# The first 489 steps of a delta-rule pipeline in an order of their own, and the preparation of the second sequence two slots earlier

## The chip, the cores and the metric

The kernel runs on one core of a Trainium2 chip. A core has five engines with instruction streams of their own, each in order: TensorE (PE; its weight loads are shown apart as PEld), VectorE (DVE), ScalarE (ACT), GpSimd (POOL) and SyncE (SP), which here issues all transfers. The metric is the device time of one execution in microseconds (us); smaller is better. Several executions are timed and the median is given; one more is profiled, and all traces come from that one.

## The reference

The input has 4 sequences of 512 rows of 256 numbers, all float32. Each sequence is normalized (layer norm). A gated delta-rule attention follows: the rows are projected to q, k, v and z, a causal convolution of four taps and a silu go over q, k and v, and per head a recurrence runs over the sequence in chunks. There are 16 q/k heads, and each serves two of the 32 v heads; a head has 128 channels. Beside it stand two numbers per row and head, beta (a sigmoid) and g (a decay), the "gates". In a chunk

```python
decay = jnp.where(tril, jnp.exp(g[..., :, None] - g[..., None, :]), 0.0)
M = jnp.where(stril, jnp.einsum('bhncd,bhnmd->bhncm', k_beta, k) * decay, 0.0)
T = solve_triangular(eye + M, eye, lower=True)
v_new = v_i - jnp.einsum('bhcd,bhde->bhce', kcd_i, state)
state = state * jnp.exp(g_last)[..., None, None] + ...
```

so every chunk needs the inverse of a triangular matrix and the state that the chunk before it left. The heads' results are normalized, multiplied by silu(z) and projected back to 256 channels (`s`). A feed-forward network whose weights are looked up in a table of 16 numbers gives `g`; the output is `x + s * silu(g)`.

## The kernel before, in words

The work is cut into 64 items: 4 sequences times 16 q/k heads, with the two v heads of each, numbered 0 to 63. An item's 512 rows are 4 chunks of 128. An item consists of some 115 named steps, each a few instructions; `STEPS` holds them. Those that matter here, in the order in which an item needs them:

- `gk`, `gq`, `gv0`, `gv1`, `gz`, `go` load weights; `g` loads the item's rows of g into the tile ds, `e` loads exp(g) into qe. These are SP's, and SP issues in order, so an issue that waits for a free buffer holds all later ones.
- `ak`, `aq`, `av0`, `av1` (L444) project on PE, `yk`... (L450) copy the last tap out on ACT, `ck0`...`cv12` (L456) are the other taps on DVE, `sk`... (L92) the silu on ACT. `z0`, `z1` project z (L478).
- `tk`, `tq`, `tv0`, `tv1` transpose on PE (L510), `sqk`, `sqq` sum squares on ACT (L503), `lk` (L88) takes logarithm and exponentials of them. Changes between the exp and the silu functions cost ACT a table load (L86, L92).
- `ds` (L495, DVE), `ls`, `x0`, `x1` (L88, ACT) make the decay; `kk0`, `kk1` (L556, PE) the products; `nt0`, `nt1` and `at0`, `at1` (L564, DVE) multiply both; `am` (L577, GpSimd) masks at; `qm` (L599, GpSimd) multiplies q into qe. `po`, which reads them, waits for both.
- The inverse: `nd` and `nl` (SP) bring the 32x32 diagonal blocks of nt through memory into a layout with one block row per partition; `yl` (ACT) sets the identity; `L0` to `L3` (L633 and L639, GpSimd) are 31 substitutions of two instructions, 62 in all; `yd` and `iu` (SP) bring the result back; `tp` (L660, DVE) transposes it; merge 1 (`m1`: W on PE L672, `wt` on ACT, U on PE L675, `iu2` on ACT, `t10` on DVE) and merge 2 (`m2`: W2 L703, `w2`, U2 L705, `iu4`) join the blocks to the inverse of 128x128. In `m1` the W of one item and the U of the item before it are interleaved instruction by instruction, in `m2` likewise.
- The recurrence: `ks`, `r`, `pv`, `vn`, `ps`, `st` and `po` for the four chunks (L729, L738, L746, L753, L759, L766, L778 and L781); then `sqo`, `so`, `ro`, `o`, `th`, `h`, and the output projection `pp0`, `pp1` (L824) with its sum `ac0`, `ac1` (L836) on DVE.

The items are pipelined by a string `SLOT` of 122 entries. Entry `pp1:13` says that slot n does step pp1 of item n - 13; `ak:1` that it does ak of item n - 1. A slot thus does one item's worth of work, taken from up to 14 items, and there are 64 slots and 14 more. The first slots have few steps, because the items that they would serve do not exist yet. The order in which the steps are called is written down, and at the end of the kernel every instruction is tied to the one before it on its engine: each engine runs in exactly that order, and one that waits holds all behind it.

Two other things are mixed in. An `X` in the string does one step of the table lookup of the feed-forward weights (two DVE instructions, L334 and L333; `lookups()` begins a new table with L326 to L330 and stores the old one), from slot 6 on; there are four a slot. A `Y` adds one to `due`, and `prepare()`, called behind every step, does one part of the preparation of the next sequence as long as `due` is above zero and two memory banks are free: `normed` (load of x, statistics on DVE, rs on ACT, scaling on DVE, transposes on PE L213, copy on ACT, a store) and then `gated` (ba on PE L233, softplus on DVE and ACT, the running sum gsum on PE, exponentials on ACT, gT on PE, and stores of g and exp(g) into memory). The preparation of sequence b + 1 begins at item 8 of sequence b; that of sequence 0's gates is spread over the first steps.

Every tile has a number of buffers (`NBUF`): two for wk, yl, nl and yd, three for nt and v1, four for q and qe, five for at and kd, nine for k, one where nothing is said (wq, the loads of v, ds, r and the lookup's tiles).

Of the kernel before, what the change touches and what calls it, by code (L numbers as in the profile page):

```python
# [15 lines left out]
B, S, D = 4, 512, 256  # L16
HQK, HV, HD = 16, 32, 128
# [21 lines left out]
def gated_delta_ffn_kernel(  # L39
# [359 lines left out]
    STEPS = {}  # L399
# [266 lines left out]
    def merge1(it, pred):  # L666
        pu = pred and pred.put("pU")[:, : G * Q].rearrange("p (g i) -> p g i", g=G)
        pw = it and it.put("pW")[:, : G * Q].rearrange("p (g i) -> p g i", g=G)
        for g in range(G):
            if it:  # L670
                for lo, hi in HALVES:
                    nc.tensor.matmul(pw[hi, g, :], lhsT=it.nt[lo, g, hi], rhs=it.tpl[lo, g, :Q], start=True, stop=True)  # L672
            if pred:
                for lo, hi in HALVES:
                    nc.tensor.matmul(  # L675
                        pu[lo, g, :], lhsT=pred.wt[hi, g, :], rhs=pred.iut[hi, g, hi], start=True, stop=True
                    )
# [20 lines left out]
    def merge2(it, pred):  # L698
        pu = pred and pred.put("pU2").rearrange("p (g i) -> p g i", g=G)
        pw = it and it.put("pW2").rearrange("p (g i) -> p g i", g=G)  # L700
        for g in range(G):
            if it:
                nc.tensor.matmul(pw[HI, g, :], lhsT=it.nt[LO, g, HI], rhs=it.tpl[LO, g, :], start=True, stop=True)  # L703
            if pred:
                nc.tensor.matmul(  # L705
                    pu[LO, g, :], lhsT=pred.w64[HI, g, :], rhs=pred.iut[HI, g, HI], start=True, stop=True
                )
# [146 lines left out]
    def feed_forward():  # L854
# [125 lines left out]
        "av0:6 at0:5 ck2:1 tv0:8 yl:5 at1:5 sqo0:10 ps0:9 yv0:6 st0:9 cv00:6 th1:11 nl:5 L3:6 av1:4 "  # L980
        "th0:11 sqo1:10 yd:6 vt0:8 tv1:7 am:9 h1:11 cv01:6"
    )
    plan = [(name, int(lag or 0)) for name, _, lag in (key.partition(":") for key in SLOT.split())]
    MERGES = {"m1": merge1, "m2": merge2}
    lags = dict(plan)
    last_lag = max(lag + (name in MERGES) for name, lag in plan)
    total = HQK * B
    looked = lookups()
    preparing = gated(0)
# [5 lines left out]
    spare, needed = 0, None  # L995
    traced = nc.cur_bb.bb.instructions
    begin = traced[-1]
    items, kept, slot = [], [], 0

    def item(n):  # L1000
        return items[n] if 0 <= n < total else None

    def feed():

        nonlocal spare, needed
        while needed is not None and spare >= needed and len(free) > 2:
            spare -= needed
            needed = next(feeding, None)

    def both(b):  # L1010
        yield from normed(b)
        yield from gated(b)

    due = 0

    def prepare():

        nonlocal due
        if due and len(free) > 1:
            due -= 1  # L1020
            while next(preparing, None):
                pass

    for n in range(total + last_lag):
        if n < total:
            items.append(Item(n))
            b, hq = divmod(n, HQK)
            if hq == HQK // 2 and b + 1 < B:
                for _ in preparing:
                    pass  # L1030
                due = 0
                preparing = both(b + 1)
        if n == total + 6:
            for _ in looked:
                pass
            needed = next(feeding)
        slot = n
        for name, lag in plan:
            if name == "X":
                if n >= 6:  # L1040
                    next(looked, None)
            elif name == "Y":
                due += 1
            elif name in MERGES:
                if item(n - lag) or item(n - lag - 1):
                    MERGES[name](item(n - lag), item(n - lag - 1))
            elif item(n - lag):
                STEPS[name](item(n - lag))
                due += n < 4 and name[0] in "ac"
                prepare()  # L1050
            elif needed is not None:
                spare += PASSES.get(name, 0)
                feed()
    slot = total + last_lag
# [53 lines left out]
```

## Time and profile before

| | us |
|---|---|
| median of three timed executions | 2072.44 (2071.39 to 2076.25) |
| the profiled execution | 2075.89 |
| its span in the trace | 2073.7 |
| PE busy | 1969.2 |
| DVE busy | 1775.5 |
| ACT busy | 1621.0 |
| GpSimd busy | 1388.5 |
| first substitution of item 0 (L633) | at 53.9 |
| first output projection (L824) | at 246.5 |
| last substitution (item 63, L639) | at 1860.3 |

Busy times are unions over an engine's instructions and leave out the short pauses between them: GpSimd's 62 instructions of an item are busy for some 19 us and take 23 to 24. The profiled execution took 3.45 us more than the median. In rows of instructions the columns are the start, the duration, the engine, the line, the operation, what it writes and reads, and in brackets the idle time before it with what ended it. In a list of waits the three numbers are the total, the count and the longest. In a table of stretches each engine has its busy time and its number of instructions, then come the granted clock of PE, the share of the transfer engines and GB/s.

### The profile page before, as it was taken

The page shows a single profiled execution, that of the slowest core. Times are in us where ns is not written, and L with a number is a line of the kernel's source. Part 1 is how long each engine was busy: PE and PEld are TensorE (multiplying, and loading weights), DVE is VectorE, ACT ScalarE, POOL GpSimd, SP SyncE. Part 2 cuts the span into 40 slices and gives each one's busy share as a digit, 9 for nine tenths or more (in the row PEclk, how much of TensorE's full clock was granted, in tenths as well). Part 3 has the DMA queues.
Part 4 walks back from the last instruction along what each step waited for, and adds up shares of the span by engine and source line. Part 5 has one row for each costly group of instructions (what it writes and reads, how often), then busy time and mean ns, then how long its engine had stood idle before and what let it go on. Part 6 is the DMA issues. An engine that isn't in the chain of part 4 may idle for free.

```text
span 2073.7 us, 48691 instructions
## 1 busy us (share of the span) xinstructions
PE 1969.2 (95%) x15744; PEld 1442.6 (70%) x15744; DVE 1775.5 (86%) x4356; ACT 1621.0 (78%) x4689; POOL 1388.5 (67%) x4181
## 2 busy tenths in 40 slices
PE   6468999999999999999999999999999999998999
PEld 3235777777777777777777777777777777775755
DVE  7788999999999999999998999999999988862323
ACT  5467889888888888888888888888888989963321
POOL 0777777777777767777777767777777777780000
PEclk9779999999999999999999999999999999999999
DMA  2343443344433444334443344443344343321211
GB/s 76 98 107 89 123 106 103 96 108 120 116 103 100 105 111 105 104 100 110 123 108 101 91 119 103 112 105 102 97 113 123 104 108 100 100 75 44 71 51 51
DMA packets 371885, 206.40 MB, mean 100 GB/s; under 512 B 224544, under 2 KB 353712, under 8 KB 371632
## 3 DMA queue, kind: packets, MB, share of 16 engines
q1 hardware_dynamic: 371632, 203.29, 37.3%
q8 instruction: 126, 2.06, 0.4%
q14 instruction: 127, 1.04, 0.2%
HBM read 179.05 MB, written 24.13 MB: 98 GB/s over the span
## 4 chain that ended last, share of the span: by engine, by line
PE 73%; DVE 16%; POOL 3%; ACT 3%; DMA 3%; issue 1%; SPq 1%; DVEq 0%; POOLq 0%; ACTq 0%
PE av L444 9%; PE pp L824 8%; PE pz L478 7%; PE pv L746 5%; PE po L781 4%; PE ak L444 4%; PE pgu L907 4%; PE kk L556 4%; PE po L778 3%; PE aq L444 3%; PE ps L759 3%; PE ks L729 3%; PE th L510 2%; PE pW L703 2%; PE ptv L510 2%; DVE v L456 2%
## 5 line engine op out<-in xcount | busy, mean ns | idle before, releaser
L633 POOL TENSOR_TENSOR pr<-nl,yl 128x60 f32<-128x60 f32 (+24 forms) x1984 | 584.0, 294 | 220.7 <-ACT ik L88 47.6
L639 POOL TENSOR_TENSOR yl<-yl,pr 128x60 f32<-128x60 f32 (+24 forms) x1984 | 605.1, 305 | 155.7 <-DMA yd<-yl 0.4
L456 DVE SCALAR_TENSOR_TENSOR v<-av,cw,v 128x509 f32<-128x509 f32 (+2 forms) x384 | 282.4, 735 | 0.6 <-ACT v L450 0.3
L478 PE MATMUL pz<-xnT,wz 128*128 128x512 f32 x512 | 242.4, 596 | 4.4 <-DVE acc L836 2.5
L824 PE MATMUL pp<-wo,zT 128*128 128x256 f32 x1024 | 243.7, 381 | 0.5 <-DVE zT L816 0.2
L444 PE MATMUL av<-xnT,wv 128*128 128x512 f32 x512 | 241.3, 594 | 1.4 <-DMA wv<-in_w_qkvz 1.4
L824 PEld LDWEIGHTS pp<-wo,zT 128*128 128x128 f32 x1024 | 185.0, 190 | 25.2 <-issue 2.9
L599 POOL TENSOR_TENSOR qe<-qe,q 128x384 f32<-128x384 f32 x128 | 126.3, 1008 | 100.6 <-DMA qe<-eg_rows 52.3
L86 ACT ACT_TABLE_LOAD x128 | 164.2, 1283 | 3.1 <-PEq L1098 0.8
L92 ACT ACT_TABLE_LOAD x128 | 164.2, 1283 | 2.3
L88 ACT ACTIVATE ds<-ds,ls 128x128 f32<-128x128 f32 x512 | 156.9, 390 | 8.2 <-DVE ls L532 6.6
L738 DVE SCALAR_TENSOR_TENSOR r<-ks,neg,vt 128x128 f32<-128x128 f32 x384 | 116.0, 343 | 44.7 <-PE ks L729 42.9
L456 DVE SCALAR_TENSOR_TENSOR q<-aq,cw,q 128x509 f32<-128x509 f32 (+2 forms) x192 | 142.3, 741 | 13.1 <-ACT q L450 10.8
L503 ACT ACTIVATE junk_o<-po 128x128 f32<-128x128 f32 x512 | 142.1, 278 | 14.3 <-PE po L781 2.1
L478 PEld LDWEIGHTS pz<-xnT,wz 128*128 128x128 f32 x512 | 95.5, 190 | 78.8 <-issue 61.2
L456 DVE SCALAR_TENSOR_TENSOR k<-ak,cw,k 128x509 f32<-128x509 f32 (+2 forms) x192 | 141.4, 736 | 2.0 <-ACT k L450 1.6
L746 PEld LDWEIGHTS pv<-r,iut 128*128 128x128 f32 x768 | 105.6, 191 | 46.0 <-issue 38.2
L444 PE MATMUL ak<-xnT,wk 128*128 128x512 f32 x256 | 135.1, 653 | 0.5 <-DMA wk<-in_w_qkvz 0.5
L444 PEld LDWEIGHTS av<-xnT,wv 128*128 128x128 f32 x512 | 87.6, 191 | 65.6 <-issue 63.9
L746 PE MATMUL pv<-r,iut 128*128 128x128 f32 x768 | 124.8, 285 | 8.4 <-DVE r L738 7.5
L444 PE MATMUL aq<-xnT,wq 128*128 128x512 f32 x256 | 120.7, 594 | 2.8 <-DMA wq<-in_w_qkvz 1.8
L495 DVE TENSOR_SCALAR ds<-ds,gc 128x128 f32<-128x128 f32 x512 | 120.9, 305 | 2.0
(177 smaller groups left out, 5058.1 us busy)
## 6 DMA issues: line engine op xcount, KB each, us to landing
ds<-g_rows SPq DMA_DIRECT2D x64, 512.0 KB, 4.0
nl<-nd SPq DMA_DIRECT2D x256, 128.0 KB, 3.9
qe<-eg_rows SPq DMA_DIRECT2D x64, 384.0 KB, 4.3
wv<-in_w_qkvz SPq DMA_DIRECT2D x128, 128.0 KB, 2.4
wz<-in_w_qkvz SPq DMA_DIRECT2D x64, 256.0 KB, 2.8
wo<-in_w_out SPq DMA_DIRECT2D x64, 256.0 KB, 3.1
wk<-in_w_qkvz SPq DMA_DIRECT2D x64, 128.0 KB, 2.5
wq<-in_w_qkvz SPq DMA_DIRECT2D x64, 128.0 KB, 2.3
```

The lines of the kernel that those rows point to most:

```text
L86: nc.scalar.preload_act_table_set("natural_log_exp_and_others")
L88: nc.scalar.activation(out, in_, func, **kw)
L92: nc.scalar.activation(out, in_, AF.Silu)
L444: nc.tensor.matmul(ps, lhsT=getattr(it, "w" + x)[:, d, :], rhs=it.xnT[:, d, :], start=(d == 0), stop=(d == DC - 1),)
L456: nc.vector.scalar_tensor_tensor(y[:, sh:], ps[:, : S - sh], cw[:, block(it.hq), j : j + 1], y[:, sh:], ALU.mult, ALU.add)
L478: nc.tensor.matmul(ps, lhsT=it.wz[:, d, p * P : (p + 1) * P], rhs=it.xnT[:, d, :], start=(d == 0), stop=(d == DC - 1),)
L503: nc.scalar.activation(junk, ps[:, c, :], AF.Square, accum_out=out[:, c : c + 1])
L599: nc.gpsimd.tensor_tensor(it.qe[:, p], it.qe[:, p], thirds(it.q, NC)[:, 1:, :], ALU.mult)
L633: nc.gpsimd.tensor_tensor(pr[:, :k, :n], nl[:, j : j + 1, j + 1 :].to_broadcast([R * LH, k, n]), yl[:, :k, j : j + 1].to_broadcast([R * LH ...
L639: nc.gpsimd.tensor_tensor(yl[:, :k, j + 1 :], yl[:, :k, j + 1 :], pr[:, :k, :n], ALU.subtract)
L746: nc.tensor.matmul(pv[:, p, :], lhsT=it.iut[:, p * NC + c, :], rhs=it.r[:, p, :] if c else vt[:, c, :], start=True, stop=True,)
L824: nc.tensor.matmul(ps[:, j, :], lhsT=chunk(hT, 2 * c2 + j), rhs=it.wo[:, p, :], start=(p == 0), stop=(p == NP - 1),)
```

## The change

A second string, `FRONT`, names 489 steps with the item of each (`L2:4` is the third part of the substitutions of item 4). They are done ahead of the loop over slots, in that order; the loop then leaves out what is done. FRONT covers about what slots 0 to 10 did and parts of 11 to 13: k of items 0 to 7, substitutions up to the third part of item 4, item 0 up to `pp1` and `ac1`. The merges are named by halves there (W, U, W2, U2), so the first W and U of items 0 to 2 stand alone and are not interleaved. The loads of `gk`, `gq`, `gv0`, `gv1`, `gz` and `go` of item 0 and `gk` of item 1 come first of all, and `yl` of items 0 and 1; `ak` of item 0 comes ahead of ba. On GpSimd qm and am of item 0 come ahead of the first substitution, qm of items 1 and 2 behind item 0's substitutions, qm of item 3 behind item 1's, am of item 1 behind item 3's. No lookup step is in FRONT.

After FRONT the loop begins at slot 0; slots 0 to 8 have no step left, slot 9 has 5, slot 10 has 13, slot 11 has 58 of 112, slot 12 has 105 of 114, and from slot 14 on all are as before. Slots 6 to 8 therefore emit their twelve lookup steps in a row. The preparation of sequence 1 begins at slot 6 instead of 8; as `prepare()` is called behind steps only, the counts of slots 6 to 8 add up and a part goes behind each step from slot 9 on. The gates of sequence 0 go behind the steps 9 to 39 of FRONT. The common order begins, on DVE, at the instruction that started at 293.7 us of the profiled execution. The number of instructions is the same on all engines but ACT, which has 252 table loads where it had 256.

```diff
+    FRONT = (
+        "yl:0 gk:0 yl:1 gk:1 gq:0 gv1:0 gv0:0 gz:0 ak:0 go:0 aq:0 yk:0 gk:2 ck0:0 ck1:0 ak:1 yq:0 gq:1 "
+        "ck2:0 cq0:0 sk:0 cq1:0 av1:0 yk:1 gk:3 cq2:0 ck0:1 sq:0 ck1:1 aq:1 yv1:0 gv1:1 ck2:1 cv10:0 sk:1 "
+        "cv11:0 kk1:0 yq:1 gq:2 cv12:0 cq0:1 tq:0 sv1:0 tk:0 cq1:1 sqq:0 ak:2 cq2:1 sqk:0 eq:0 aq:2 gk:4 "
+        "yk:2 g:0 sq:1 ck0:2 e:0 kk0:0 ck1:2 e:1 yq:2 ck2:2 gq:3 kk1:1 e:2 cq0:2 sk:2 e:3 cq1:2 av1:1 cq2:2 "
+        "lk:0 ls:0 ds:0 tq:1 yv1:1 gv1:2 tk:1 sqq:1 qm:0 ak:3 kd:0 cv10:1 sqk:1 cv11:1 kk0:1 gk:5 cv12:1 "
+        "yk:3 aq:3 eq:1 lk:1 ck0:3 x0:0 ck1:3 x1:0 ck2:3 av0:0 gq:4 yq:3 nt1:0 nt0:0 tk:2 ls:1 nd:0 at1:0 "
...
+        "po0:1 yv1:6 nd:5 po1:1 vn2:1 cv10:6 yl:5 ps2:1 cv11:6 sqo0:1 po2:1 cv12:6 iu:3 st2:1 L1:4 tq:6 "
+        "sv1:6 so0:1 ks3:1 sqq:6 tv0:3 r3:1 U2:2 nl:5 vt0:3 pv3:1 vt1:3 pp1:0 ds:6 iu4:2 vn3:1 gv1:7 tp:3 "
+        "av0:4 ro0:1 L2:4 ac1:0"
+    )
     plan = [(name, int(lag or 0)) for name, _, lag in (key.partition(":") for key in SLOT.split())]
     MERGES = {"m1": merge1, "m2": merge2}
+    HALF = {"m1": ("W", "U"), "m2": ("W2", "U2")}
+    STEPS.update({
+        "W": lambda it: merge1(it, None), "U": lambda it: merge1(None, it),
+        "W2": lambda it: merge2(it, None), "U2": lambda it: merge2(None, it),
+    })
...
+    for name, _, m in (key.partition(":") for key in FRONT.split()):
+        m = int(m)
+        while len(items) <= m:
+            items.append(Item(len(items)))
+        if (name, m) == ("g", 0):
+            for _ in preparing:
+                pass
+        done.add((name, m))
+        STEPS[name](items[m])
+        due += 8 < len(done) < 40
+        prepare()
     for n in range(total + last_lag):
...
-            if hq == HQK // 2 and b + 1 < B:
+            if hq == (HQK // 2 if b else 6) and b + 1 < B:
...
             elif name in MERGES:
-                if item(n - lag) or item(n - lag - 1):
-                    MERGES[name](item(n - lag), item(n - lag - 1))
-            elif item(n - lag):
+                it, pred = (
+                    None if (half, m) in done else item(m) for half, m in zip(HALF[name], (n - lag, n - lag - 1))
+                )
+                if it or pred:
+                    MERGES[name](it, pred)
+            elif item(n - lag) and (name, n - lag) not in done:
                 STEPS[name](item(n - lag))
-                due += n < 4 and name[0] in "ac"
                 prepare()
```

## The prediction

> **What bounds the kernel now.** First the page: totals and slices.
>
> ```profile
> PE 1969.2 (95%) x15744; PEld 1442.6 (70%) x15744; DVE 1775.5 (86%) x4356; ACT 1621.0 (78%) x4689; POOL 1388.5 (67%) x4181
> ...
> PE   6468999999999999999999999999999999998999
> PEld 3235777777777777777777777777777777775755
> DVE  7788999999999999999998999999999988862323
> POOL 0777777777777767777777767777777777780000
> ```
>
> The reader is to see that PE is full from slice 4 on, DVE too, and that only the first four slices (207 us) have room. So next the stretches of the start, and two stretches of four steady slots each behind them:
>
> ```profile
> core 0: us, PE busy (x) PEld busy (x) DVE busy (x) ACT busy (x) POOL busy (x), PEclk, DMA share, GB/s
> 25.00:54.00 29.00, 24.50 (x77) 12.82 (x78) 23.28 (x45) 22.08 (x58) 0.12 (x1) 0.88 0.35 96
> 54.00:168.00 114.00, 59.08 (x410) 35.33 (x408) 86.86 (x207) 59.18 (x166) 90.85 (x280) 0.78 0.41 105
> 168.00:257.00 89.00, 84.23 (x714) 63.43 (x714) 80.66 (x207) 76.75 (x222) 67.38 (x203) 0.97 0.39 99
> 257.00:346.00 89.00, 86.97 (x789) 64.76 (x789) 84.48 (x213) 76.02 (x222) 66.51 (x198) 1.00 0.41 107
> 346.00:458.00 112.00, 111.56 (x913) 83.52 (x900) 108.29 (x265) 98.60 (x288) 86.21 (x257) 1.00 0.41 105
> ```
>
> From 168 us on PE and DVE are both at 91 to 99%. PE paces a slot at 28 us (112 / 4), DVE needs 27.1 of them, so DVE can make up about 1 us a slot and no more. PE's room lies in 54:168, 55 us of it; DVE has 27 us there. What holds PE in that stretch is in the waits of the first 300 us:
>
> ```profile
> POOL pr L633 <- ACT ik L88: 47.6, 1, 47.6
> PEld pW L672 <- DVE tpl L660: 42.0, 6, 17.4
> PE pW L672 <- DVE tpl L660: 40.7, 6, 17.0
> ```
>
> PE waits for tp, which waits for GpSimd's substitutions. The timelines of GpSimd, DVE and PE give the marks that the sum uses:
>
> ```profile
> 53.88 0.24 POOL L633 TENSOR_TENSOR pr<-nl,yl 128x31 f32<-128x31 f32 x1 [47.58 <-ACT ik L88]
> ...
> 77.84 1.94 POOL L599 TENSOR_TENSOR qe<-qe,q 128x384 f32<-128x384 f32 x2
> 79.75 0.24 POOL L633 TENSOR_TENSOR pr<-nl,yl 128x31 f32<-128x31 f32 x1
> ...
> 43.88 1.41 DVE L564 TENSOR_TENSOR nt<-kk,ds 128x256 f32<-128x256 f32 x4
> 168.21 1.35 DVE L660 STREAM_TRANSPOSE tpl<-iut 32x256 f32<-32x256 f32 x3
> 345.47 0.22 PE L672 MATMUL pW<-tpl,nt 32*32 32x32 f32 x2
> ```
>
> One item's 62 substitutions take 24 us with their gaps, and from 53.9 us GpSimd goes from item to item almost without a pause (starts at 53.9, 79.8, 105.4, 132.7, 159.8). So the front is a chain: nt of item 0 (ends 45.3), 8.6 us through nd and nl, then 26 to 28 us an item. DVE's tp of item 3 comes at 168.2; merge 1 of item 9 on PE, which lies in the part whose order is the same in both kernels, at 345.5. I price the change at that last mark: behind it each engine has the same instructions in the same order.
>
> **Step 1, the gates of sequence 0.** ak of item 0 moves ahead of ba on PE. ba took 3.89 us and this ak 3.69, both at the cold rate, so the gate chain starts 2.1 to 3.7 us later (the low end if PE is warm by then). Back come 0.6 us (gsum no longer waits for ak) and 0.65 (no tap ahead of the copy of gT). The exp of gT, at 24.25 now, comes at 25.1 to 26.7, the evacuation of the first q 0.6 behind it. The seven weight loads that move to the front of SP's queue (0.47 us of issue each, wz and wo of 256 KB among them) lie where SP is idle, between 6.5 and 12.9 us; without that cover the store of xnT would go some 3 us later, and nobody waits for it.
>
> **Step 2, from that q to nt of item 0.** Both orders run 21 to 22 taps ahead of ds, so DVE's amount is equal; ACT's is not. By rows: evacuation 0.7, three q taps 2.25, a wait of 0.25, then taps of k1, v1 of item 0, q1 (6.75): 9.95. DVE then waits for ACT, which has a silu, the squares of q0 and k0 (1.58 a group) and an evacuation first: 12.1. Taps of k2 and q2 (4.5): 16.6. Table load 1.28 and lk 0.65, partly beside these taps: 17.0. Now x0 and x1 stand behind an evacuation, the squares of q1 and k1, another evacuation and lk of item 1: 21.9, plus 2.45 for the eight exps, plus 1.4 for nt: 25.8 us. nt of item 0 ends at 51.5 to 53.1, not 45.3. The load of ds stands on SP behind a wk that waits for ak of item 2: issued near 36, landed near 40.5 (4.0 to landing), needed at 42.5 to 44. Four loads of qe (384 KB each) follow it; aq of item 3 stands behind them and has 5 us to spare. Without that cover up to 4 us would come on top.
>
> **Step 3, first substitution.** nd and nl took 8.6 us (45.3 to 53.9). One weight load stands between them on SP (0.4). Start at 60.5 to 62.1; I take 61.3, which is **7.4 us later**. GpSimd's q product and mask of item 0 (2.0 and 1.1) now lie ahead of it, in time when GpSimd is idle.
>
> **Step 4, GpSimd to item 3.** 24.0 + 4.0 (q products 1, 2) + 23.5 + 2.0 + 23.0 + 23.7: item 3 ends 100.2 behind the start, at 161.5 (now 156.4). Now GpSimd pauses 1.84 and 0.48 us ahead of item 3; the new order has the inputs (nt of items 1 and 2, qe, yl) ready 10 us and more ahead, so I price no pause, and one of that size would come on top. yd, iu and tp followed item 0's end in 7.0 us (77.9 to 84.9): 168.5. But the mask of item 1 stands behind item 3 on GpSimd (162.6), po0 of item 1 waits for it on PE, and ks3, r3, two vt and ds stand behind po on the way to tp, about 8 us of rows: **tp of item 3 at 170.5**, between 168.5 and 172.5, against 168.2.
>
> **Step 5, DVE behind it.** Counted from the two orders, the new one has done by then 8 nt/at halves, 16 ds, 8 r, 6 state updates, 4 vt, 2 o, 2 zT and small ones more (18.5 us) and 17 lookup steps, two lookup openings and part of the norm less (14.9 + 2.7). That is 0.9 us ahead. Up to merge 1 of item 9 DVE now works 165.1 us and stands idle 12.2 (177.3 from 168.2). So 164.2 us remain, and the start's reordering has not shortened the engine that is full: it exchanged lookups for item work. The norm and gates of sequence 1 (some 7 us of DVE, 5 of PE) lie inside both stretches, now spread over slots 8 to 16, then packed into 9 to 12.
>
> **Step 6, DVE's stalls.** Slots 6 to 8 emit nothing but lookups and preparation marks, so twelve lookup steps stand in a row behind tp of item 3, and then the norm of sequence 1, a part behind each step. On PE the transposes of x follow merge 1 of item 3 at once and wait for the last scaled row: 0.65 + 1.5 + 16 x 0.75 + norm 3.4 + taps 2 + another opening 1.5 + tp itself 1.35, about 23 us of PE idle. DVE then waits for what stood behind that on PE: transposes, ak of item 9, two copies, the evacuation. The same ak took 1.88 us in a busy stretch and 3.62 behind a 3.84 us idle one, so 4.2 to 7 us. SP is held in that time too: the store of xnT stands ahead of yd of item 4, which would be ready at 188 and goes at 200; iu lands at 208, when DVE arrives as well. Between lookup tables DVE waits for the store to land (4.1 us now, once; here about 1.2). With 5 to 6 of the 12.2 us that remain in slots 11 to 15, I take 14 us, from 8 (no norm stall) to 21 (both queues hold it).
>
> **The sum.** 170.5 + 164.2 + 14 = 348.7, against 345.5; 0.7 us of it I let DVE's slack take up: **+2.5 us**. Four table loads fewer on ACT (5.1 us) lie beside idle time. PE's own work is unchanged, and 23 us of its idle time only move. In the profiled execution (span 2073.7, 2075.9 with what lies around it) that makes 2078.4; that execution is 3.5 above the median of the three, so against 2072.44 I say **2075**.
>
> Here one rule speaks against the change. The Trainium skill, SBUF — State Buffer, "Who interferes with whom", says that a VectorE instruction with two SBUF inputs excludes a GpSimd instruction that reads SBUF for its whole length. The twelve adds in a row would, by it, each cost GpSimd or DVE up to 0.3 us (one substitution's row), 3.6 in all, an estimate. In the rows of before the adds (L333) take 0.50 to 0.59 us beside a busy GpSimd, and item 0's substitutions, beside a half idle DVE, took 24.0 us against 23.2 beside a full one; so no charge is made for it.
>
> **Rivals.**
> Faster: GpSimd alone decides. From 61.3, items 0 to 6 end at 61.3 + 164.3 + 12.4 = 238.0, merge 1 of item 6 could follow in 8.3 us (item 2's now; usually 16) at 246.3 against 257.0, and three slots of 28 lead to 330 to 334: 11 to 15 us gained, 2059. For it: PE has over 20 us of room there. Against it: it needs DVE to stall 0, and DVE's 164 us do not fit between 170.5 and 334. A part of it (nt at 50, tp at 167, 8 us of stall) gives 2066.
> Slower: the norm in one burst. If each of its exchanges between DVE, ACT and PE (statistics, rs, transposes, ba, softplus, gsum, gT) holds DVE for 2 to 3 us and yd of item 4 goes late, nt of item 6 (which also needs a buffer that merge 2 of item 3 frees) passes 215 and GpSimd runs dry for 6 us or more. From there every us is lost, because no later slot has more than 1 us of slack: 20 to 25 us of stalls, 2082 to 2090. For it: today these parts go two a slot with half a slot between. Against it: most are separated by a step.
> No effect: the lag at slot 13 is the same to 3 us and the steady order takes it up: 2072.
>
> **How the numbers follow.** Forecast (−3.5 to +9.2 us by stalls of 8 to 21): 0.40. No effect: 0.10. Faster rival, whole or in part: 0.20. Slower rival: 0.30. A change under 0.3% (6.2 us) is about what a measurement here cannot tell from none: the slower side has the slower rival and 0.04 of the forecast, less 0.02 of the rival's low end, the faster side the faster rival and 0.02 of the forecast: 0.22, 0.46, 0.32. The range 2062 to 2088 cuts the best half of the faster rival and the worst third of the slower one, 2 in 10; the forecast's own is 2069 to 2082.
>
> **What would show it.** Right: first L633 at 60 to 63 us; L660 of item 3 at 168 to 173; PE idle for some 20 us ahead of a second group of L213 near 195, released by DVE xs; merge 1 of item 9 at 343 to 352; the same 28 us a slot behind it. Wrong: a first substitution before 57 us, merge 1 of item 6 before 252 (faster) or behind 266 (slower), or another slot length.

## The result, and the profile after

Seven executions of each kernel on one chip: before 2073.23 us (2071.39 to 2076.25), after **2079.29** (2077.35 to 2080.15). The ratio is 1.0027, 95% interval 1.0015 to 1.0038: slower by some 6 us, just below what the prediction called measurable. The profiled executions took 2075.89 and 2080.06, their spans are 2073.7 and 2078.1. The prediction said 2075, between 2062 and 2088.

The page of after, totals and slices of 52 us:

```profile
PE 1977.6 (95%) x15744; PEld 1446.0 (70%) x15744; DVE 1777.5 (86%) x4356; ACT 1615.1 (78%) x4685; POOL 1387.5 (67%) x4181
...
PE   6685899999999999999999999999999999998999
PEld 3453577777777777777777777777777777775755
DVE  7877999999999999999999999999999988862323
POOL 1778478777777777778776767777777777780000
```

PE's second and third slices went from 4 and 6 to 6 and 8 and its fourth from 8 to 5, GpSimd's fifth from 7 to 4. From slice 6 on no digit changes by more than one: room was moved, not removed. The same four stretches as shown of before:

```profile
core 0: us, PE busy (x) PEld busy (x) DVE busy (x) ACT busy (x) POOL busy (x), PEclk, DMA share, GB/s
25.00:54.00 29.00, 22.62 (x84) 12.27 (x84) 25.93 (x49) 23.54 (x75) 2.03 (x2) 0.94 0.43 120
54.00:168.00 114.00, 90.22 (x629) 59.55 (x629) 85.66 (x206) 79.10 (x223) 88.44 (x290) 0.88 0.38 98
168.00:257.00 89.00, 56.88 (x443) 37.98 (x442) 77.05 (x187) 41.30 (x123) 56.03 (x161) 0.83 0.30 73
257.00:346.00 89.00, 87.08 (x727) 64.75 (x726) 85.73 (x210) 78.38 (x226) 69.60 (x210) 1.00 0.43 114
```

In 54:168 PE works 90 us where it worked 59; in 168:257 it works 57 where it worked 84. PE's gain of 31 us in the front is given back by 27 directly behind it. DVE, the column to watch, has no gain in either: 85.66 for 86.86, 77.05 for 80.66. What PE and GpSimd wait for in 168 to 262 us, the list of waits:

```profile
PE tpx L213 <- DVE xs L204: 21.2, 2, 17.5
POOL qe L599 <- DMA qe<-eg_rows: 20.8, 1, 20.8
```

Before's list of that stretch has no wait for xs, and 3.0 us for qe. The marks, from the timelines of GpSimd, DVE and PE:

```profile
58.89 0.24 POOL L633 TENSOR_TENSOR pr<-nl,yl 128x31 f32<-128x31 f32 x1 [2.04 <-DMA nl<-nd]
...
228.78 1.95 POOL L599 TENSOR_TENSOR qe<-qe,q 128x384 f32<-128x384 f32 x2 [20.82 <-DMA qe<-eg_rows]
...
169.71 1.36 DVE L660 STREAM_TRANSPOSE tpl<-iut 32x256 f32<-32x256 f32 x3
202.34 0.75 DVE L456 SCALAR_TENSOR_TENSOR k<-ak,cw,k 128x509 f32<-128x509 f32 x1 [5.43 <-ACT k L450]
...
191.51 0.84 PE L213 MATMUL tpx<-ident,xs 128*128 128x128 f32 x2 [17.46 <-DVE xs L204]
353.29 0.22 PE L672 MATMUL pW<-tpl,nt 32*32 32x32 f32 x2
```

The first substitution comes 5.0 us later than before, tp of item 3 1.5 later, merge 1 of item 9 **7.8 us** later (353.3 for 345.5). At the end of item 63's substitutions 5.2 of these are left (1865.5 for 1860.3), in the span 4.4.

For the experiments one sum is made from the rows of each trace: from tp of item 3 to merge 1 of item 9, the time in which at least one VectorE row runs ("work"), and the rest ("idle"). Between these marks before had 164.4 + 12.9 us, after 168.1 + 15.5. All columns but the last are of the one profiled execution, the last is the median of several. "Lookups" are the sixteen steps that the string SLOT gives to slots 6 to 9, 14.4 us at 0.9 each.

| kernel | tp of item 3 | work | idle | merge 1 of item 9 | PE waits for xs | median |
|---|---|---|---|---|---|---|
| before | 168.2 | 164.4 | 12.9 | 345.5 | 0 | 2073.2 |
| after | 169.7 | 168.1 | 15.5 | 353.3 | 21.2 | 2079.3 |
| norm from slot 8 | 168.0 | 167.9 | 13.9 | 349.8 | 19.8 | 2078.3 |
| lookups from slot 10 | 167.7 | 152.0 | 14.8 | 334.5 | 5.6 | 2066.0 |
| both | 174.1 | 152.0 | 14.1 | 340.2 | 3.9 | 2067.3 |
| before, lookups from slot 10 | 162.8 | 164.9 | 13.3 | 340.9 | 0 | 2069.8 |
| lookups in waits | 172.2 | 154.3 | 15.2 | 341.8 | 8.4 | 2068.2 |
| lookups spread | 173.6 | 154.4 | 15.0 | 343.0 | 8.4 | 2071.2 |
| lookups doubled | 171.3 | 183.5 | 15.7 | 370.5 | 37.4 | 2095.8 |
| q product of item 1 early | 167.1 | 167.1 | 15.1 | 349.3 | 20.4 | 2075.9 |
| the same, lookups from slot 10 | 164.4 | 151.5 | 18.6 | 334.5 | 5.6 | 2064.6 |
| and item 0 early | 165.8 | 152.2 | 15.7 | 333.6 | 5.7 | 2061.8 |
| and its mask later | 164.9 | 151.7 | 16.2 | 332.8 | 5.8 | 2063.7 |
| and lookups from slot 14 | 165.3 | 138.7 | 21.0 | 325.0 | 3.8 | 2060.7 |

The marks have a spread of their own. Five kernels of the table (after, norm from slot 8, lookups from slot 10, both, lookups doubled) have the same PE, VectorE, ScalarE and GpSimd instructions in the same order up to tp of item 3, and the same SP issues up to 3 us ahead of it, and still tp came at 169.7, 168.0, 167.7, 174.1 and 171.3. The granted clock of PE in 54:168 was 0.88, 0.93, 0.94, 0.85 and 0.88 there; whether it makes the spread or follows from it, these runs don't tell. The earliest and the latest, "lookups from slot 10" and "both":

```profile
54.00:168.00 114.00, 88.39 (x641) 58.12 (x641) 89.35 (x216) 82.08 (x228) 87.46 (x286) 0.94 0.40 99
54.00:168.00 114.00, 90.07 (x593) 58.34 (x592) 82.61 (x198) 76.13 (x207) 88.26 (x289) 0.85 0.36 92
```

The first of these is the fastest of its five timed executions (2062.4, median 2066.0), the second the slowest of its five (2069.5, median 2067.3). So differences of a few us at tp, and at merge 1 of item 9 as far as they stand at tp already, are no effect of an edit by themselves. Work and idle time behind tp don't contain them.

### The profile page after: what moved, and what is told of

Read it like the earlier page. It is cut to its first block, busy times and chain, and to the rows that moved or that the text cites. A ratio compares the mean times of both kernels' runs of the same rounds, so it can differ in the third digit from the quotient of the medians.

```text
span 2078.1 us, 48696 instructions
## 1 busy us (share of the span) xinstructions
PE 1977.6 (95%) x15744; PEld 1446.0 (70%) x15744; DVE 1777.5 (86%) x4356; ACT 1615.1 (78%) x4685; POOL 1387.5 (67%) x4181
## 4 chain that ended last, share of the span: by engine, by line
PE 76%; DVE 16%; ACT 2%; POOL 2%; DMA 2%; issue 1%; SPq 1%; DVEq 0%; POOLq 0%; ACTq 0%
PE pp L824 9%; PE av L444 9%; PE pz L478 8%; PE pv L746 5%; PE po L781 4%; PE ak L444 4%; PE kk L556 4%; PE aq L444 4%; PE pgu L907 4%; PE po L778 3%; PE ps L759 3%; PE ks L729 3%; PE th L510 2%; PE pW L703 2%; PE ptv L510 2%; PE pd L956 2%
## 5 line engine op out<-in xcount | busy, mean ns | idle before, releaser
L456 DVE SCALAR_TENSOR_TENSOR v<-av,cw,v 128x509 f32<-128x509 f32 (+2 forms) x384 | 282.3, 736 | 6.7 <-ACT v L450 5.8
L444 PE MATMUL av<-xnT,wv 128*128 128x512 f32 x512 | 246.1, 604 | 4.2 <-ACT ds L88 2.0
L738 DVE SCALAR_TENSOR_TENSOR r<-ks,neg,vt 128x128 f32<-128x128 f32 x384 | 116.0, 343 | 46.7 <-PE ks L729 44.8
L456 DVE SCALAR_TENSOR_TENSOR q<-aq,cw,q 128x509 f32<-128x509 f32 (+2 forms) x192 | 142.3, 741 | 13.4 <-ACT q L450 10.9
L503 ACT ACTIVATE junk_o<-po 128x128 f32<-128x128 f32 x512 | 142.0, 277 | 15.1 <-PE po L781 2.8
L456 DVE SCALAR_TENSOR_TENSOR k<-ak,cw,k 128x509 f32<-128x509 f32 (+2 forms) x192 | 141.4, 736 | 8.9 <-ACT k L450 8.3
L444 PE MATMUL ak<-xnT,wk 128*128 128x512 f32 x256 | 130.7, 634 | 0.9 <-ACT lk L88 0.6
L495 DVE TENSOR_SCALAR ds<-ds,gc 128x128 f32<-128x128 f32 x512 | 122.1, 308 | 1.9
```

The source lines that it names most:

```text
L444: nc.tensor.matmul(ps, lhsT=getattr(it, "w" + x)[:, d, :], rhs=it.xnT[:, d, :], start=(d == 0), stop=(d == DC - 1),)
L456: nc.vector.scalar_tensor_tensor(y[:, sh:], ps[:, : S - sh], cw[:, block(it.hq), j : j + 1], y[:, sh:], ALU.mult, ALU.add)
L503: nc.scalar.activation(junk, ps[:, c, :], AF.Square, accum_out=out[:, c : c + 1])
```

## The experiments

The question was why after loses although PE has over 20 us of waiting in slots 6 to 9. Three theories: the norm of sequence 1, brought forward into one burst, makes the engines wait for each other; the lookups, which now stand in a row behind tp of item 3, are VectorE work added where VectorE is the bound; or neither matters, because work that is moved costs the same elsewhere. The expectations call them A, B and D; their rival C is the late start of the substitutions.

**The norm back to slot 8, in after.**

```diff
-            if hq == (HQK // 2 if b else 6) and b + 1 < B:
+            if hq == HQK // 2 and b + 1 < B:
```

> The new kernel with one part undone: the preparation of sequence 1 begins at slot 8 again, the listed front stays. Theory A (VectorE is the full engine; what the front could give is lost where the norm of sequence 1 stands in one burst behind a row of lookups, so that PE waits 17.5 and 3.7 us for the scaled rows and VectorE then waits back): the transposes of x wait under 6 us, merge 1 of item 9 comes at 343 to 348 us instead of 353.3, the time is 2069 to 2075. Rival B (the loss is the 16 lookup steps in a row themselves, which stand there whatever the norm does): merge 1 of item 9 stays at 351 to 355 and the time at 2077 to 2081. Rival C (the late start of the substitutions, 58.9 against 53.9, is the loss): also 2077 to 2081, since that start does not change.

Measured: 2078.33 (2073.68 to 2079.31), ratio to before 1.0016 (1.0007 to 1.0024). PE still waits once for xs, and in one piece:

```profile
PE tpx L213 <- DVE xs L204: 19.8, 1, 19.8
```

VectorE's idle time falls by 1.6 us and merge 1 of item 9 comes 3.5 earlier; 1.7 of these stand at tp of item 3 already, ahead of which nothing differs. The time keeps 1.0, within the spread. The mark lies between the forecasts of theory A and rival B, the time and PE's wait are those of B. The early norm is at most a small part of the loss.

**The lookups from slot 10 on**, in after, in the kernel of the run above, and in before.

```diff
             if name == "X":
-                if n >= 6:
+                if n >= 10:
                     next(looked, None)
```

> The new kernel with the table lookups from slot 10 instead of 6; the norm stays early. Theory A: without lookups between tp of item 3 and the norm the transposes of x wait some 5 us instead of 21, and 14 us of VectorE work leave the stretch up to merge 1 of item 9, which comes at 331 to 340 us; the lookups end four slots later (slots 62 to 66), where VectorE has room for part of them: 2062 to 2071. Rival B (16 lookups in a row are the loss): the same sign, as large or larger. Rival D (VectorE is full to the end, so work moved to the end costs there what it saved here): merge 1 of item 9 earlier by 13 us or more, the time within 4 us of the new kernel, 2075 to 2083.

> Both at once: norm of sequence 1 from slot 8, lookups from slot 10. Theory A: no burst and no lookups ahead of slot 10, merge 1 of item 9 at 330 to 338 us, the time 2058 to 2068, and 2 to 8 us below the kernel with the late lookups alone. Rival B: no better than the kernel with late lookups alone (within 2 us). Rival D: within 4 us of the new kernel.

> The kernel before with nothing changed but the lookups, from slot 10 instead of 6. It tells whether late lookups are a gain of their own. Theory A: in the old order VectorE stands idle 27 us between 54 and 168 us while it waits for GpSimd, so lookups there cost little: merge 1 of item 9 up to 6 us earlier, the time 2066 to 2074. If the lookups held the start back: merge 1 of item 9 earlier by 10 us or more and the time 2058 to 2064. If VectorE is full to the end: 2074 to 2080.

Measured: 2066.0 (ratio 0.996, 0.9948 to 0.9973), 2067.3 (0.9968, 0.9956 to 0.9981) and 2069.76 (0.9984, 0.9975 to 0.9993). In after the edit gives 13.3 us (17.7 between the profiled executions) and takes 18.8 from merge 1 of item 9, as A and B forecast. The stretch 168:257 of after with this edit, to be set against the third row of after above:

```profile
168.00:257.00 89.00, 71.87 (x614) 49.18 (x613) 76.58 (x187) 55.78 (x165) 68.98 (x211) 0.92 0.34 89
1650.00:1750.00 100.00, 99.38 (x897) 75.42 (x896) 94.06 (x242) 90.07 (x267) 77.28 (x233) 1.00 0.39 101
```

PE does 15 us more there while VectorE is as busy as before: the same VectorE time now carries item work. The second row is where the lookups went: VectorE is 94 of 100 busy near the end (88 in after) and PE no less full. So work that is moved does not cost the same, and the third theory (rival D) falls. In before the same edit gives only 3.5 us. The table says why: there those sixteen steps lay ahead of tp of item 3, among waits; taken out, tp comes 5.4 us earlier and the work behind it does not change. After had put them behind tp, 14.4 us of them into a stretch whose idle time stays at 13 to 16 us in all kernels but two.

What the written order is worth by itself lies between kernels with late lookups: before's order 2069.8, the listed one 2066.0 with the norm from slot 6 and 2067.3 with the norm from slot 8, as before has it. That is 2.5 to 3.8 us in its favour; the intervals of the first pair are apart, those of the second overlap a little. So the lookups cost some 10 us more behind tp than where before had them (13.3 against 3.5), the order gives back up to 4, and the loss of 6 is left. With late lookups the norm from slot 6 is no loss (2066.0 against 2067.3; idle time behind tp 14.8 against 14.1): B's forecast, not A's. The 5.7 us between the marks of these two stand at tp already.

**The lookups elsewhere in the front, and doubled.** `X` becomes a name that FRONT may hold, sixteen of them in each of two versions; in the third, slots 6 to 9 do two steps at each X.

```diff
+        if name == "X":
+            next(looked, None)
+            continue
...
-                if n >= 6:
+                if n >= 10:
                     next(looked, None)
```

```diff
                 if n >= 6:
                     next(looked, None)
+                if 6 <= n < 10:
+                    next(looked, None)
```

> The kernel after, with its first sixteen lookup steps taken out of slots 6 to 9, where they stand in a row behind the transposes of item 3, and put into the stated order where VectorE waits in the trace of after: one (only a load) ahead of the q transpose of item 1, six ahead of the q taps of item 5 (7.2 us of waiting at 76.9), one ahead of the v transposes at 96.0 (1.4 us), two ahead of the negated products of item 3 at 115.7 (2.3 us), three ahead of the v taps of item 5 at 119.9 (2.9 us), one at 136.4 (1.7 us), two ahead of the v taps of item 6 at 162.5 (2.6 us). No lookup is moved to the end of the kernel. If the row of lookups is the cause: merge 1 of item 9 starts at 338 to 343 (353.3 in after, 334.5 with the lookups from slot 10 on), the 21 us that TensorE waits for the norm's transposes fall below 8, and the time is 2064 to 2068, a little under the 2066.0 of the kernel that starts them in slot 10, since the last slots are one row lighter. If those waits cannot be filled, because the waiting instructions behind them are only pushed back (loads of the indices stand on SyncE's queue as well): merge 1 of item 9 at 348 or later and 2074 or more.

> The kernel after, with the same sixteen lookup steps spread over the last half of the stated order, one behind every thirteen steps from the transposes of item 0 on (127 to 170 us), where VectorE is 90 of 100 busy; none in a row, none moved to the end, none put into a wait on purpose. If the sum of VectorE's work ahead of merge 1 of item 9 decides (14.4 us of lookups, of which the waits of 127 to 170, 5 to 6 us, may take some): merge 1 of item 9 at 346 to 352 and 2072 to 2078. If only standing in a row right ahead of the norm decides: merge 1 of item 9 at 337 to 342 and 2064 to 2068. If the front is tighter than the slots behind it: 354 or later and 2080 or more.

> The kernel after with the suspected cost doubled: each of the sixteen lookup steps of slots 6 to 9 takes the one that follows it along, so that 32 stand there in a row, and the lookups end four slots sooner. If VectorE's work ahead of merge 1 of item 9 adds up in full: merge 1 of item 9 at 353.3 + 14.4 = 367.7 (366 to 370), TensorE's wait for the norm's transposes 21 + 14 = 35 us, and 2079.3 + 13 = 2092 (2089 to 2095). If half of it falls into waits that are there anyway: 359 to 362 and 2084 to 2088. If the row is not the cause: 353 to 356 and 2078 to 2082.

Measured: 2068.16 (0.9975, 0.9964 to 0.9985), 2071.21 (0.9984, 0.9975 to 0.9993) and 2095.76 (1.0103, 1.0089 to 1.0117). The stretch 54:168 of the one with the lookups in waits, where VectorE had 85.66 us in after:

```profile
54.00:168.00 114.00, 87.74 (x606) 56.81 (x605) 97.97 (x235) 78.56 (x218) 87.99 (x279) 0.90 0.38 96
```

It takes 12.3 us more of VectorE work and tp of item 3 comes 2.5 us later. Merge 1 of item 9 is where the first case of its forecast had it (341.8; 338 to 343 expected), the time 0.2 above its upper edge, PE's wait 0.4 above its bound. The spread version met neither forecast: 343.0 lies between 337 to 342 and 346 to 352, and 2071.2 between 2064 to 2068 and 2072 to 2078. The order in a row is no cause by itself, nor does every us count wherever it stands: in that version VectorE's idle time ahead of tp of item 3 was 34.9 us, where the five kernels with the listed order had 40.7 to 47.4 (after 43.1), so about 8 of the 14 us went into waits. Aiming at the waits won 1.2 us of merge 1 more, which the spread of tp does not tell from nothing.

Doubling adds 17.2 us to merge 1 of item 9 and 16.5 to the time, a little over the 14.4 of the steps and just above the forecast's upper edges (370 and 2095): 15.4 more of work, with one more table begun and stored, and tp of item 3 1.6 later. PE's wait grows from 21.2 to 37.4, of which 33.3 in one piece:

```profile
209.04 0.48 PE L213 MATMUL tpx<-ident,xs 128*128 128x128 f32 x1 [33.29 <-DVE xs L204]
```

So PE's wait measures VectorE's backlog, and work added to VectorE behind tp of item 3 goes into the time in full.

**GpSimd's q product of item 1 ahead of item 0's substitutions.** This undoes the one move on GpSimd that a wait in the trace of after spoke against: VectorE waited 7.2 us at 76.9 for a q buffer of item 1, free only when that product is done.

```diff
-        "lk:0 ls:0 ds:0 tq:1 yv1:1 gv1:2 tk:1 sqq:1 qm:0 ak:3 ...
+        "lk:0 ls:0 ds:0 tq:1 yv1:1 gv1:2 tk:1 sqq:1 qm:0 qm:1 ak:3 ...
...
-        "... L3:0 qm:1 qm:2 ds:2 ...
+        "... L3:0 qm:2 ds:2 ...
```

> The kernel after, with GpSimd's q product of item 1 put back to where its operands come ready, right behind that of item 0 and ahead of item 0's substitutions (in after it stands behind them, at 81.4). The 7.2 us that VectorE waits at 76.9 for the q taps of item 5, and the 11.3 us of TensorE at 89.6 behind them, should go. If the front's own waits count in the time: merge 1 of item 9 2 to 6 us earlier than the 353.3 of after and a time of 2073 to 2077. If the row of lookups in slots 6 to 9 sets the time whatever stands ahead of it, since VectorE catches up at it: merge 1 of item 9 at 352 to 354 and 2077 to 2081. If the product ahead of the substitutions delays these by its 2 us and they are the chain: 355 or later and 2081 or more.

> The kernel after with two of its moves undone at once: the lookups from slot 10 on (alone 2066.0, merge 1 of item 9 at 334.5), and GpSimd's q product of item 1 ahead of item 0's substitutions (alone 2075.9, merge 1 of item 9 at 349.3, where after has 353.3). If VectorE's work and waits ahead of merge 1 of item 9 add up, the two gains add: 334.5 - 4.0 = 330.5, and 2066.0 - 3.4 = 2062.6, between 2061 and 2064.5. If the second gain came from a wait that the lookups' row had lengthened, it is gone with the row: merge 1 of item 9 at 333.5 to 335 and 2065 to 2068.

Measured: 2075.9 (1.001, 1.0001 to 1.0019), merge 1 of item 9 at 349.3, the first case of its forecast. The wait is gone. Together with late lookups: 2064.63 (0.9952, 0.9939 to 0.9966), and merge 1 of item 9 unmoved at 334.5. There tp of item 3 comes 3.3 us earlier and VectorE's idle time behind it grows by 3.8: at the mark the gains do not add, the second forecast, while the time lies between the two. In the five kernels of the table with this product early tp stands at 164.4 to 167.1, in the five that share the listed order at 167.7 to 174.1, so it comes earlier in all of them. What that is worth in the time is not clear of noise: the interval of 2075.9 overlaps after's, that of 2064.63 the one of 2066.0.

**Item 0's decays and products early, then its mask later, then lookups from slot 14.** All on top of the last kernel.

```diff
-        "lk:0 ls:0 ds:0 tq:1 ... kd:0 cv10:1 ... x0:0 ck1:3 x1:0 ... nt1:0 nt0:0 tk:2 ls:1 nd:0 ...
+        "lk:0 ls:0 ds:0 x0:0 x1:0 tq:1 ... kd:0 nt1:0 nt0:0 nd:0 cv10:1 ...
```

```diff
-        "... nd:0 cv10:1 ... av1:2 nl:0 sq:2 cv01:0 am:0 ... L3:0 ...
+        "... nd:0 nl:0 cv10:1 ... av1:2 sq:2 cv01:0 ... L3:0 am:0 ...
```

```diff
-                if n >= 10:
+                if n >= 14:
                     next(looked, None)
```

> The one before this, with item 0's decays, negated products and their store moved ahead of the taps and sums of squares of items 1 to 3, so that the first substitution starts 3 to 6 us earlier (62 with the q product of item 1 moved ahead, 58.9 in after, 53.9 before). If VectorE's sum decides and the substitutions follow: the time of the one before this within 2 us, merge 1 of item 9 too, and the gain shows as a longer GpSimd wait further back. If the start of the substitutions is the front's chain: merge 1 of item 9 and the time 3 to 5 us earlier (2057 to 2060).

> The one with item 0's decays and negated products early, with two more steps moved: the load of item 0's negated products directly behind their store, and GpSimd's mask of item 0's attention products, which waited there for VectorE to 61.3, from ahead of item 0's substitutions to behind them. The first substitution should start at 54 to 57 (62.7 with the mask ahead of it). If the front's chain runs through the substitutions: merge 1 of item 9 at 327 to 330 and 2056 to 2059. If VectorE and TensorE set it: merge 1 of item 9 at 332 to 335 and 2060 to 2064, and the substitutions of items 0 to 3 end some 6 us earlier for nothing.

> The one before this with the lookups from slot 14 on: sixteen more of VectorE's lookup steps (14.4 us) go from slots 10 to 13 to the other end of the kernel, where VectorE was 94 of 100 busy in 1650 to 1750 and 79 in 1750 to 1850. If VectorE's sum still sets merge 1 of item 9: it starts 10 to 14 us earlier, and the time falls by 5 to 14 unless the end takes it back. If with the first sixteen steps gone TensorE sets it (it has nearly no idle time from 230 us on): merge 1 of item 9 within 3 us and the time within 3. If the end has no room left for sixteen more: 3 us or more above the one before this.

The first of these did not do what it was to do. GpSimd's timeline:

```profile
61.28 1.09 POOL L577 TENSOR_SCALAR_AFFINE_SELECT at<-at 128x1024 f32<-128x1024 f32 x1 [14.30 <-DVE at L564]
62.70 0.24 POOL L633 TENSOR_TENSOR pr<-nl,yl 128x31 f32<-128x31 f32 x1 [0.32 <-DMA nl<-nd]
```

The mask, which stands ahead of the substitutions, waited for VectorE instead. With mask and load moved as well the first substitution starts at 56.3:

```profile
56.33 0.24 POOL L633 TENSOR_TENSOR pr<-nl,yl 128x31 f32<-128x31 f32 x1 [10.26 <-DMA nl<-nd]
```

For these 6.4 us merge 1 of item 9 moves by 0.8. Times: 2061.84 (0.9937, 0.9924 to 0.9949) and 2063.74 (0.9956, 0.9942 to 0.9969), the second as forecast for VectorE and PE setting the mark. The start of item 0's substitutions is not on the front's chain. But the gain is lost on GpSimd already: it waits 4.2 us for the blocks of item 1, and item 3's substitutions start only 1.2 us earlier (132.8 for 134.0), not the 6 expected. A front in which all four items' substitutions come earlier was not run. Why the first of the two is 2.8 us below the kernel that it was made from, with merge 1 of item 9 moved by 0.9, stays open; the intervals overlap.

The lookups from slot 14 on: 2060.72 (0.9942, 0.9929 to 0.9954), merge 1 of item 9 7.8 us earlier; VectorE's work falls by 13.0 and its idle time grows by 4.8: part of the gain now goes into waits for other engines, and the mark lies between the forecasts (10 to 14 earlier, or within 3). The time, 3.0 lower, is the second one's, and the two intervals overlap. Of the 7.8 us, 7.0 are left at merge 1 of item 30, 4.8 at item 55 and 1.4 at item 63. This kernel and the one of 2061.84 are the best, 0.6% below before; which of them is faster the intervals don't tell. What takes the gain back in the middle was not followed.

## Why the prediction was right or wrong

The measured 2079.3 lies in the range and in the forecast's own (2069 to 2082). The forecast's mechanism, VectorE full up to merge 1 of item 9 and its work only exchanged, held: over the table VectorE's work behind tp runs from 138.7 to 183.5 us, and its idle time stays at 13 to 16 in all kernels but two. It came out 4.6 us short at merge 1 of item 9 (+3.2 forecast, +7.8 measured).

*Steps 1 to 3.* nt of item 0 ended at 51.4 (51.5 to 53.1 forecast), the first substitution came at 58.9 (60.5 to 62.1), because nd and nl took 7.5 us where 9 were charged. That this start decides little is shown by item 3, whose substitutions start at 132.4 in after and at 132.7 in before, and by the run with the start at 56.3, though with late lookups only.

*Step 4.* tp of item 3 at 169.7; 170.5 was forecast, in its range of 168.5 to 172.5. That it lies so near is luck. Item 3's substitutions ended at 154.9 where 161.5 was forecast: the first began 2.4 us earlier, and an item took some 22.5 us where 23 to 24 were charged. The last iu landed at 165.9, and VectorE came to tp 3.8 us behind that, with no wait right ahead of it. So tp stood in VectorE's own queue, and 6.6 us too much for GpSimd hid 5.8 too little behind it. Not foreseen was the wait of 7.2 us behind the q product of item 1. It is a term that the step should have had: the change moves GpSimd's products, and the q buffers' users stand behind them.

*Step 5, the term that was off most.* 164.2 us of VectorE work were forecast to merge 1 of item 9; the trace has 168.1. (The 165.1 us of before from which this was counted are those of 168 to 346 us; between the marks it had 164.4.) The number of instructions was right, their durations not: 3.2 of the 3.9 us are five rows behind tp of item 3 that ran over 0.3 us longer than the median of their kind, all beside GpSimd's q products: two of the lookups (1.4 us) and three small adds of L794 (1.8). Before has none in that stretch. The prediction had weighed just this and made no charge, by rows beside substitutions, which take 0.24 us each; a q product takes 1.0. Its 0.50 to 0.59 us for the adds left out rows that before's trace has: ahead of tp of item 3 two rows of lookups run beside a q product and take 1.13 and 0.76 us, where the median is 0.39 (L334) and 0.50 (L333):

```profile
103.48 1.13 DVE L334 TENSOR_SCALAR lt_g<-fx_g,lut_b 128x344 f32<-128x344 f32 x1
131.78 0.76 DVE L333 TENSOR_TENSOR lw_g<-lw_g,lt_g 128x344 f32<-128x344 f32 x1
```

VectorE and GpSimd in the trace of after, at the row of lookups:

```profile
179.99 0.39 DVE L334 TENSOR_SCALAR lt_g<-fx_g,lut_b 128x344 f32<-128x344 f32 x1
180.41 1.19 DVE L333 TENSOR_TENSOR lw_g<-lw_g,lt_g 128x344 f32<-128x344 f32 x1
181.52 1.12 DVE L334 TENSOR_SCALAR lt_g<-fx_g,lut_b 128x344 f32<-128x344 f32 x1
182.68 0.52 DVE L333 TENSOR_TENSOR lw_g<-lw_g,lt_g 128x344 f32<-128x344 f32 x1
...
180.10 2.35 POOL L599 TENSOR_TENSOR qe<-qe,q 128x384 f32<-128x384 f32 x2
182.41 0.33 POOL L633 TENSOR_TENSOR pr<-nl,yl 128x31 f32<-128x31 f32 x1
```

The add and the product with a constant take 1.19 and 1.12 us for as long as the two q products run, 0.52 and 0.39 ahead and behind. No run moved the q products away from these rows; the 3.2 us are read from the rows alone.

*Step 6.* 14 us of idle time, from 8 to 21, against 15.5. PE's wait for xs was forecast at about 23 us near 195 and was 21.2 at 191.5 and 196.1; VectorE's wait behind it at 4.2 to 7 and was 5.4. SP's hold of yd of item 4 came too, for 22 us (item 4 done at 180.1, sent at 202.2) where 12 were priced. What the step did not see is that the PE wait was no cost by itself; VectorE works through it.

*The sum.* −0.8 (tp), +3.9 (work) and +1.5 (idle) make the 4.6. The slots behind gave back 2.6 us, not 0.7. The rest of the distance, +6.1 in the medians against +4.2 in the profiled executions, is the executions' own spread.

*The signs.* Of the signs of being right, three came: tp of item 3, PE's idle time near 195 released by xs, and 28.2 us a slot behind merge 1 of item 9. Two did not: the first substitution (58.9; 60 to 63 stated) and merge 1 of item 9 (353.3; 343 to 352 stated). Merge 1 of item 6 came at 267.3, behind the 266 that was the sign of the slower rival. So by its marks the kernel lies between forecast and slower rival; the time, 2079.3, lies in the forecast's own range and 3 us short of the rival's.

*The rivals.* GpSimd alone deciding: merge 1 of item 6 at 267.3, not 246, as VectorE never had the room. The burst of the norm: its signs came, nt of item 6 at 221.2 (215 was the mark) and GpSimd dry for 20.8 us, but its price did not: VectorE idled 15.5 us, not 20 to 25, and with the norm back at slot 8 one us of time was won. The signs belong to VectorE's backlog, 14.4 us of it lookups, which the prediction had counted in step 5 and not named as a rival. No effect: 7.8 us of lag was not taken up.

## What to carry to other kernels

Where one in-order engine is full, ask of every step that a reordering moves on which side of that engine's waits it lands: here sixteen side steps, moved from a stretch with 45 us of waits into one with little to spare, cost 13 us where they had cost 3.5, and the better order of 489 steps gained 4 at most. A wait of another engine that grows with this engine's queue is the backlog's measure, not the cause; taking the suspect out and doubling it (−19 and +17 us at the same mark) tells the two apart. Before reading a mark of one execution, see how far it moves between kernels that are the same up to it: 6.4 us here. Price contention by rows beside the same instruction, not beside a shorter one of the same engine.

## What the runs showed of the hardware

**VectorE rows beside a long GpSimd row.** With the q product of item 1 placed behind that of item 0, four of them run in a row, beside VectorE's ds. VectorE and GpSimd:

```profile
44.27 3.91 DVE L495 TENSOR_SCALAR ds<-ds,gc 128x128 f32<-128x128 f32 x8
...
43.25 3.87 POOL L599 TENSOR_TENSOR qe<-qe,q 128x384 f32<-128x384 f32 x4 [36.96 <-ACT lk L88]
```

Eight ds rows, 1.7 to 2.0 us elsewhere in this trace, take 3.9: the first three 1.02 each, the length of a q product. Over the whole trace of after, rows that start beside a q product take, on average, 0.87 us for 0.30 (L495, 3 rows), 0.96 for 0.47 (L333, 2 rows) and 0.54 for 0.16 (L794, the 20 rows that start with over 0.15 us of the product left; each of them ends 0.015 to 0.020 us behind the product's end). Rows with an input in PSUM are unchanged: the taps take 0.73 for 0.74 (L456, 45 rows) and r 0.35 for 0.34 (L738, 84 rows). The Trainium skill, SBUF — State Buffer, "Who interferes with whom", states this distinction: a VectorE instruction with two SBUF inputs, or in a two-port mode, which it gives as possible for tensor_scalar, contends with GpSimd for ports that one of the two holds for its whole instruction while the other is blocked; one with at most one SBUF input outside these modes does not contend. The rows agree with it. GpSimd can be the one that waits: its second substitution row takes 0.46 to 0.49 us beside the lookups' adds at 178 to 184, where it took 0.25 at 59.

**SP's order and GpSimd.** GpSimd's 20.8 us without work in after end with a load of exp(g), whose issue stands on SP behind the store nd of item 6; that store waits for VectorE's nt, which is late by the lookups. With the lookups from slot 10 on, item 6's substitutions start at 213.2, with them in slots 6 to 9 at 231.1, doubled at 249.1.
